# Two graph-attention layers on one core: where the fills of layer 0 end, how the first pair of heads sums its rows, and how far m^T is loaded ahead

## The chip, the cores and the metric

The kernel runs on one core of one Trainium2 chip. A core has a matrix engine (TensorE, PE in the profile, its weight loads PEld), a vector engine (VectorE, DVE), an activation engine (ScalarE, ACT), GpSimd (POOL) and a sync engine (SP) that here only issues DMAs. The engines run side by side and wait for each other on semaphores. The metric is the device time of one execution in microseconds, the median over several runs. Lower is better.

## What is computed

The input is x, eight images (B = 8) of 2048 nodes with 256 channels, and one adjacency matrix of 2048 x 2048 that all images share. Two layers follow each other, each with a residual and a layer norm. Cut to what matters:

```
def layer0(x, adj, W, a_src, a_dst, beta_tilde, W_out):     # 8 heads of width 32
    x_proj = einsum('bnd,hdf->bhnf', x, W)
    e = leaky_relu(e_src[..., :, None] + e_dst[..., None, :], 0.2)
    e = e + softplus(beta_tilde) * log(prior + 1e-6)          # prior = adj
    e = where(adj > 0, e, -max)
    h = einsum('bhij,bhjf->bhif', softmax(e), x_proj)
    return merge_heads(h) @ W_out.T

def layer1(x, adj, W1, W2, W3):
    e = leaky_relu((x @ W1) @ (x @ W2).T, 0.2)
    e = where(adj > 0, e, -1e12)
    return relu(softmax(e) @ (x @ W3))

x = layernorm(x + layer0(x, adj, ...))
x = layernorm(x + layer1(x, adj, ...))
```

All of it is computed in float32.

## The kernel before, in words

**Layer 0.** The score of a pair of nodes depends on one number of the query and one of the key, so exp(leaky_relu(...)) becomes a maximum of two products. The kernel never forms the scores. For one head and one tile of 128 keys (jt, sixteen of them) the vector engine makes a tile `s` of 128 keys x 2048 queries with one instruction: the maximum of a query row `c` and a number per key, times a tile of `m^T` (the masked adjacency factor, transposed, the same for all heads and images). That is L382. The matrix engine then multiplies `s` by the 32 columns of values of that head, which gives the numerator `val`, and by a column of key weights, which gives the row sum `den`. Both are made by `products` (L411 to L414): four matmuls side by side, each on 32 columns of the array, one for each block of 512 queries. [...] one call of `products` is eight matmul records.

The row sums can also be made on the other engines. For key tiles named in `SUMMED` (L68) there is no matmul for `den`. Instead the first of them is scaled into a tile `d` by ACT (L398), each later one is added to `d` by the vector engine (L393), and at the end of the pair one call of `products` with a tile of ones adds `d` into `den` (L405). This trades a call of `products` for a vector instruction.

The heads are taken in pairs. A unit is one key tile for one pair of heads: two `s` tiles, two calls for `val`, up to two for `den`. A pair has 16 units, an image four pairs, so 64 units. `step(count)` (L347) does `count` units. `val` and `den` have one buffer each, so the first `val` product of the next pair must wait until ACT has copied the old `val` out: eight copies (L428) and one for `den` (L430).

**Layer 1.** `Dot` works on blocks of 128 queries, sixteen for an image. A step of it transposes the weights of block it (L580, copied out by ACT, L582), makes the scores of block it+1 (L554, evicted by ACT, L556), has the vector engine apply the mask and take the maximum (L559), has ACT take the exponential (L562), and multiplies the transposed weights by `h3` into `acc` (L596). Transposes and scores share three PSUM tiles (`mm_tile`).

**How the two are put together.** The loop at the end (L684) runs layer 1 of image b-1 against layer 0 of image b. `dot.step(fill)` calls `fill(1)` after its `acc` matmuls (L597), and the fill there is a number of layer 0 units. The first pair of an image (pair 0) has its units in a fill of four (L700) and in the stretch in which the output projection of the previous image is made (L709 to L718, `output` and `turn`); that is 16 units. Two fills of two follow (L722). The remaining 44 units are spread evenly over 13 steps by the division in L725: 3, 3, 4, 3, 3, 4, 3, 4, 3, 3, 4, 3, 4. Pairs 1 and 2 therefore end inside a fill. Pair 3 ends with one.

**Loads.** The order on the matrix engine and, in this loop, on the SP queue is the order in which the program is written. The vector engine's and ACT's orders are made by the compiler's scheduler. SP issues all large loads in turn and waits at an issue until the tile's buffer is free, so what stands behind it waits too. A tile of `m^T` is 1 MB and is loaded anew for each unit (L206 to L209). Two buffers carry the tag `mt`. Two more carry the tag `d`; they hold the row-sum tiles, and in places also `m^T` tiles. `load_ahead` (L322) sets up the loads, and L386 decides after each unit whether one more is issued: two tiles ahead in general, four where a pair has no row sum chain and jt is below 12. The `s` tiles come from a ring of eight buffers, shared with the weights `p` of layer 1 and one half of the heads' output `ht`.

Of the kernel before, what the change touches and what calls it, by code (L numbers as in the profile page):

```python
# [27 lines left out]
def kernel(  # L28
# [27 lines left out]
    B, N, D = x.shape  # L56
    H, _, DH = w_proj.shape
    NT = N // P
# [5 lines left out]
    NP = H // HP  # L64
# [1 line left out]


    SUMMED = [[()] * NP, [()] + [(0, 3, 6, 8, 11, 14)] * (NP - 1)]  # L68
    SUMMED += [[(0, 4, 10, 13)] + [tuple(range(0, NT, 2))] * (NP - 1)] * (B - 2)

    const = ctx.enter_context(tc.tile_pool(name="const", bufs=1))
    dram = ctx.enter_context(tc.tile_pool(name="dram", bufs=1, space=DRAM))
# [10 lines left out]
    def ring_tile(name, shape=(P, N)):  # L83


        return wide.tile(list(shape), F32, tag="s", name=name, bufs=8)

    def wide_tile(name, tag, bufs, dtype=F32):
        return wide.tile([P, N], dtype, tag=tag, name=name, bufs=bufs)
# [113 lines left out]
        nc.sync.dma_start(mt_d[ts(jt, P), :], mt)  # L203
        return mt

    def load_mt(jt, deep):  # L206
        mt = wide_tile("mt", "d" if deep and jt % 2 else "mt", 2)
        nc.sync.dma_start(mt, mt_d[ts(jt, P), :])
        return mt  # L209

# [29 lines left out]
    class Gat:  # L240
# [81 lines left out]
        def load_ahead(self):  # L322


            self.mt_loads = (load_mt(jt, b == self.b and hp == 0)
                             for b in range(self.b, B) for hp in range(NP) for jt in range(NT))
            self.c_loads = (gats[b].query_rows(h) for b in range(self.b, B) for h in range(H))
            self.mts, self.cs_ahead = [], []
            for _ in range(HP):
                self.cs_ahead.append(next(self.c_loads))  # L330
                self.mts.append(next(self.mt_loads))
            for _ in range(2):
                self.mts.append(next(self.mt_loads))

        def follow(self, gat):
# [11 lines left out]
        def step(self, count=1):  # L347

            for _ in range(count):
                hp, jt = next(self.units)  # L350
                for work in list(self.later):
                    if next(work, self) is self:
                        self.later.remove(work)
                if hp == NP - 1 and jt == 0 and self.b + 1 < B:
                    gats[self.b + 1].load_factors()

                at = self.b * NP + hp + 1
                if at < B * NP:
                    gat = gats[at // NP]
                    if jt == 4 and gat.b > 0:  # L360
                        gat.load(at % NP)
                    elif jt == 12:
                        gat.scale(at % NP)
                if jt == 0:
                    if self.b > 0:
                        self.cs = [self.cs_ahead.pop(0) for _ in range(HP)]
                    else:
                        self.cs = [self.query_rows(hp * HP + a) for a in range(HP)]
                    self.val = pacc.tile([P, HALF], F32, tag="val", name="val")
                    self.den = pacc.tile([P, HALF], F32, tag="den", name="den")  # L370
                first = self.b == 0 and hp == 0
                if first:
                    self.more_mt(jt + 2, jt > 0)
                if self.b > 0:
                    mt = self.mts.pop(0)
                else:
                    mt = self.mts[jt] if first else load_mt(jt, True)
                s = []
                for a in range(HP):
                    h = hp * HP + a  # L380
                    sa = ring_tile("s")
                    nc.vector.scalar_tensor_tensor(sa, self.cs[a], self.re[:, 0, jt, h:h + 1], mt, ALU.max, ALU.mult)  # L382
                    s.append(sa)
                    if self.b > 0 and jt == NT - 1:
                        self.cs_ahead += [c for c in [next(self.c_loads, None)] if c]
                if self.b > 0 and len(self.mts) < (4 if not SUMMED[self.b][hp] and jt < NT - 4 else 2):  # L386
                    self.mts += [t for t in [next(self.mt_loads, None)] if t]
                v, e = self.v[hp], self.re[:, 1]
                heads = [hp * HP + a for a in range(HP)]
                chain = SUMMED[self.b][hp]  # L390
                if jt - 1 in chain[1:]:
                    for d, sa, h in zip(self.sums, self.last, heads):
                        nc.vector.scalar_tensor_tensor(d, sa, e[:, jt - 1, h:h + 1], d, ALU.mult, ALU.add)  # L393
                self.last = s
                if jt in chain[:1]:
                    self.sums = [wide_tile("d", "d", 2) for _ in heads]
                    for d, sa, h in zip(self.sums, s, heads):
                        nc.scalar.activation(d, sa, AF.Copy, scale=e[:, jt, h:h + 1])  # L398
                for a, h in enumerate(heads):
                    self.products(self.val, a, v[:, jt, ts(a, DH)], s[a], jt == 0, jt == NT - 1)  # L400
                    if jt not in chain:
                        self.products(self.den, a, e[:, jt, h:h + 1].to_broadcast([P, DH]), s[a],
                                      jt == min(set(range(NT)) - set(chain)), not chain and jt == NT - 1)
                    if chain and jt == NT - 1:
                        self.products(self.den, a, ones, self.sums[a], False, True)  # L405
                if jt == NT - 1:
                    work = self.finish(hp)
                    next(work)
                    self.later.append(work)
# [259 lines left out]
    count = (B - 1) * NT  # L669
# [14 lines left out]
    for b in range(1, B + 1):  # L684
        gat, fresh = gats[b - 1], gats[b] if b < B else None

        def layer_0(count):
            if fresh:
                fresh.step(count)

        if b > 1 and fresh:
            fresh.follow(gat)
        rows, turns = gat.output(), gat.turn()
        if dot is None:
            layer_0(4)
            next(projections)
            next(rows)
        else:

            dot.step(lambda k: layer_0((0, 4)[k]))  # L700
            if not fresh:
                for work in gat.later:
                    for _ in work:
                        pass
            next(rows)
            dot.step()
        layer_0(2)

        for g in range(NB + 2):  # L709
            if g < NB:  # L710
                next(rows)
            if g > 1:
                next(turns)
                if g == NB + 1:
                    dot = Dot(gat)
                next(turns)
            if g < NB + 1:
                layer_0(2)  # L718
        dot.scores(0)
        for _ in turns:  # L720
            pass
        dot.step(lambda k: layer_0((2, 2)[k]))  # L722
        count = NP * NT - 20
        for i in range(NT - 3):
            n = (i + 1) * count // (NT - 3) - i * count // (NT - 3)  # L725
            dot.step(lambda k: layer_0((0, n)[k]))
    dot.step()
    dot.step()
# [29 lines left out]
```

## Time and profile before

| | before |
|---|---|
| median of 3 runs | 4395.74 us (4391.2 to 4400.43) |
| the profiled execution, its own time | 4392.72 us |
| its span, first to last instruction | 4390.9 us |
| PE busy | 4163.8 us, 95% |
| DVE busy | 3697.2 us, 84% |
| ACT busy | 1714.5 us, 39% |
| DMA | 843.49 MB, mean 192 GB/s |
| mean granted TensorE clock | 0.983 |

The span has three parts. Up to about 500 us the first image goes through layer 0 alone while the projections of the other images are made. From there to about 4050 us layer 1 of one image runs against layer 0 of the next, seven times; the later rounds repeat each other every 512 us. The last 340 us are layer 1 of the last image alone, in which the vector engine is busy for a fifth of the time. A busy share is a mean over these parts. What an edit is worth is read from the part in which its instructions stand, and from the wait that ends last there. "Idle before" is time in which an engine stood still ahead of an instruction, with the instruction of the other engine that ended it.

### The profile page before, as it was taken

How to read it: one execution, taken by the hardware profiler on the slowest of the kernel's cores; microseconds unless marked ns; L12 is line 12 of the kernel's file. 1: busy time of each engine (PE TensorE's matmuls, PEld its weight loads, DVE VectorE, ACT ScalarE, POOL GpSimd, SP SyncE). 2: the span in 40 equal slices, each digit the busy share in tenths (PEclk: the TensorE clock that was granted, in tenths of full speed). 3: DMA queues.
4: the chain of work that ended last, by engine and by line, in shares of the span. 5: the costliest groups of instructions: out<-in, count | busy, mean ns of one | idle time of the engine just before them, and what ended most of it. 6: DMA issues, size and time to landing. Idle time of an engine off the chain costs nothing.

```text
span 4390.9 us, 58737 instructions
## 1 busy us (share of the span) xinstructions
PE 4163.8 (95%) x24640; PEld 2221.5 (51%) x24640; DVE 3697.2 (84%) x2468; ACT 1714.5 (39%) x3211; POOL 7.5 (0%) x14
## 2 busy tenths in 40 slices
PE   7999999999999999999999999999999999999999
PEld 4444454445545445454545445454454545455666
DVE  6878878998998989989899989989899898999222
ACT  6522243332444333343433324343333334333554
POOL 0000000000000000000000000000000000000000
PEclk9999999999999999999999999999999999999999
DMA  7988756566555555556554564555554555543211
GB/s 242 308 272 308 274 189 214 210 224 214 184 187 185 200 202 182 172 185 212 190 194 177 186 205 178 187 189 199 198 182 165 191 208 195 189 173 142 80 49 41
DMA packets 272553, 843.49 MB, mean 192 GB/s; under 512 B 33184, under 2 KB 166304, under 8 KB 198560
## 3 DMA queue, kind: packets, MB, share of 16 engines
q1 hardware_dynamic: 236448, 806.17, 52.3%
q10 hardware_dynamic: 35840, 33.57, 2.2%
q8 instruction: 193, 3.16, 0.3%
q14 instruction: 72, 0.59, 0.0%
HBM read 763.76 MB, written 75.37 MB: 191 GB/s over the span
## 4 chain that ended last, share of the span: by engine, by line
PE 62%; DVE 19%; issue 6%; ACT 6%; DMA 3%; SPq 0%; ACTq 0%; DVEq 0%
PE e L554 15%; PE acc L596 15%; PE val L414 13%; DVE s L382 11%; PE den L414 8%; DVE d L393 4%; PE pt L580 4%; ACT ht L428 3%; PE h1p L543 2%; PE y L483 2%; DMA mt<-mt_d 2%; PE proj L274 2%; DVE p L559 1%; PE h3p L522 1%; ACT d L398 1%
## 5 line engine op out<-in xcount | busy, mean ns | idle before, releaser
L382 DVE SCALAR_TENSOR_TENSOR s<-c,re,mt 128x2048 f32<-128x2048 f32 x1024 | 2360.7, 2341 | 124.6 <-DMA mt<-mt_d 52.4
L414 PE MATMUL val<-s,v 128*32 128x512 f32 x8192 | 1039.4, 609 | 122.7 <-ACT ht L428 74.1
L554 PE MATMUL e<-x1t,h 128*128 128x512 f32 x2048 | 974.1, 600 | 22.7 <-ACT pts L582 21.6
L596 PE MATMUL acc<-h,pts 128*128 128x256 f32 x4096 | 905.0, 379 | 0.0
L596 PEld LDWEIGHTS acc<-h,pts 128*128 128x128 f32 x4096 | 777.6, 190 | 156.6 <-issue 57.4
L393 DVE SCALAR_TENSOR_TENSOR d<-s,re,d 128x2048 f32<-128x2048 f32 x318 | 739.0, 2344 | 25.2 <-ACT d L398 25.2
L414 PE MATMUL den<-s,re 128*32 128x512 f32 x5216 | 684.5, 597 | 0.0
L414 PEld LDWEIGHTS val<-s,v 128*32 128x32 f32 x8192 | 243.6, 111 | 716.5 <-issue 480.4
L559 DVE CUSTOM_DVE_ANT_0 p<-p,pen 128x2048 f32<-128x2048 f32 x128 | 292.9, 2288 | 287.0 <-ACT p L556 287.0
L554 PEld LDWEIGHTS e<-x1t,h 128*128 128x128 f32 x2048 | 354.7, 192 | 287.3 <-issue 253.6
L556 ACT ACTIVATE p<-e 128x512 f32<-128x512 f32 x512 | 305.2, 596 | 432.7 <-PE e L554 424.3
L562 ACT ACTIVATE p<-p,neg 128x2048 f32<-128x2048 f32 x128 | 256.5, 2004 | 447.3 <-DVE neg L559 447.3
L580 PEld LDWEIGHTS pt<-ident,p 128*128 128x128 f32 x2048 | 249.5, 142 | 303.6 <-issue 251.8
L582 ACT COPY pts<-pt 128x512 f32<-128x512 f32 x512 | 296.4, 584 | 214.9 <-PE pt L580 201.6
L414 PEld LDWEIGHTS den<-s,re 128*32 128x32 f32 x5216 | 169.9, 111 | 393.6 <-issue 393.6
L580 PE MATMUL pt<-ident,p 128*128 128x128 f32 x2048 | 313.1, 278 | 10.4 <-ACT p L562 7.1
L230 ACT ACTIVATE f<-mv,eps_ln 128x1 f32<-128x1 f32 x128 | 37.8, 295 | 517.4 <-DVE mv L228 517.4
L428 ACT COPY ht<-val 32x512 f32<-32x512 f32 x256 | 147.8, 577 | 129.8 <-PE val L414 127.0
L601 ACT ACTIVATE z<-acc,rec 128x256 f32<-128x256 f32 x128 | 60.4, 472 | 241.0 <-PE acc L596 143.1
L274 PE MATMUL proj<-wp,xt 128*128 128x272 f32 (+1 forms) x512 | 133.7, 406 | 5.5 <-ACT both L278 2.4
L602 DVE TENSOR_TENSOR z<-z,x1r 128x256 f32<-128x256 f32 x128 | 53.9, 421 | 89.1 <-ACT z L601 89.1
L483 PE MATMUL y<-wot,ht 128*128 128x256 f32 x512 | 123.4, 396 | 1.9 <-ACT x1t L517 1.9
(88 smaller groups left out, 1980.3 us busy)
## 6 DMA issues: line engine op xcount, KB each, us to landing
mt<-mt_d SPq DMA_DIRECT2D x496, 1024.0 KB
c<-c_d SPq DMA_DIRECT2D x64, 1024.0 KB
pen<-pen_d SPq DMA_DIRECT2D x112, 512.0 KB
xg<-in_x_dram SPq DMA_DIRECT2D x60, 512.0 KB
adj_t<-in_adj_dram SPq DMA_DIRECT2D x16, 1024.0 KB
mt_d<-mt SPq DMA_DIRECT2D x16, 1024.0 KB
rb<-rec_d SPq DMA_DIRECT2D x128, 128.0 KB
x_d<-ht ACTq DMA_DIRECT2D x64, 256.0 KB
```

Of the source, the lines that this page charges most:

```text
L274: nc.tensor.matmul(t[:, 0:cols], xt[kc][:, ts(it % IG, P)], wp[:, kc, 0:cols], start=(kc == 0), stop=(kc == KC - 1))
L382: nc.vector.scalar_tensor_tensor(sa, self.cs[a], self.re[:, 0, jt, h:h + 1], mt, ALU.max, ALU.mult)
L393: nc.vector.scalar_tensor_tensor(d, sa, e[:, jt - 1, h:h + 1], d, ALU.mult, ALU.add)
L414: nc.tensor.matmul(dst[ts(q, DH), ts(a, BK)], weights, s[:, ts(q, BK)], start=start, stop=stop)
L428: nc.scalar.copy(ht[ds(lo + a * DH, DH), ts(q, BK)], self.val[ts(q, DH), ts(a, BK)])
L554: nc.tensor.matmul(t, self.h1[:, kc, ts(it % IG, P)], self.x1t[:, kc, ts(c, BK)], start=(kc == 0), stop=(kc == KC - 1))
L556: nc.scalar.activation(p[:, ts(c, BK)], t, AF.Prelu, alpha=ALPHA)
L559: nc.vector.tensor_tensor_reduce(p, p, pen, -1.0, FMAX, ALU.add, ALU.min, neg)
L562: nc.scalar.activation(p, p, AF.Exp, bias=neg, scale=-1.0, accum_out=den)
L580: nc.tensor.transpose(t[:, ts(k, P)], p[:, ts(g * IG + k, P)], ident)
L582: nc.scalar.copy(pt, t)
L596: nc.tensor.matmul(acc, pts[g][:, ts(k, P)], self.h3[:, j, :], start=(j == 0), stop=(j == NT - 1))
```

## The change

Three edits, all in the loop of rounds.

- The fills are written out as a list, 4, 4, 4, 3, 3, 3, 3, 4, 3, 3, 3, 3, 4, again 44 units in 13 steps. Now pairs 1 and 2 also end where a fill ends.
- In images 2 to 7 the first pair has no row sum chain: `SUMMED` had tiles 0, 4, 10 and 13 there. Image 1 had none in its first pair already.
- Tiles 4, 5, 8 and 9 of `m^T` of every first pair are loaded into buffers with the tag `d`, and up to four tiles are loaded ahead from jt = 2 to jt = 9. Before, this was so for image 1 alone, with every odd tile. At the start two tiles are loaded instead of four. Image 0 keeps its alternation; only the call is written otherwise.

```diff
-    SUMMED += [[(0, 4, 10, 13)] + [tuple(range(0, NT, 2))] * (NP - 1)] * (B - 2)
+    SUMMED += [[()] + [tuple(range(0, NT, 2))] * (NP - 1)] * (B - 2)
...
-    def load_mt(jt, deep):
-        mt = wide_tile("mt", "d" if deep and jt % 2 else "mt", 2)
+    def load_mt(jt, tag="mt"):
+        mt = wide_tile("mt", tag, 2)
         nc.sync.dma_start(mt, mt_d[ts(jt, P), :])
         return mt
...
-            self.mt_loads = (load_mt(jt, b == self.b and hp == 0)
+            self.mt_loads = (load_mt(jt, "d" if hp == 0 and jt in (4, 5, 8, 9) else "mt")
                              for b in range(self.b, B) for hp in range(NP) for jt in range(NT))
...
             for _ in range(HP):
                 self.cs_ahead.append(next(self.c_loads))
-                self.mts.append(next(self.mt_loads))
-            for _ in range(2):
                 self.mts.append(next(self.mt_loads))
...
-                    mt = self.mts[jt] if first else load_mt(jt, True)
+                    mt = self.mts[jt] if first else load_mt(jt, ("mt", "d")[jt % 2])
...
-                if self.b > 0 and len(self.mts) < (4 if not SUMMED[self.b][hp] and jt < NT - 4 else 2):
-                    self.mts += [t for t in [next(self.mt_loads, None)] if t]
+                if self.b > 0:
+                    ahead = 2 if hp > 0 or not 1 < jt < 10 else min(4, 11 - jt)
+                    while len(self.mts) < ahead and (mt := next(self.mt_loads, None)):
+                        self.mts.append(mt)
...
-        count = NP * NT - 20
-        for i in range(NT - 3):
-            n = (i + 1) * count // (NT - 3) - i * count // (NT - 3)
+        for n in (4, 4, 4, 3, 3, 3, 3, 4, 3, 3, 3, 3, 4):
             dot.step(lambda k: layer_0((0, n)[k]))
```

## The prediction

> **What bounds the kernel now.** I read the busy rows first (PE 95%, DVE 84%), then the chain that ended last, then the windows of one repeated round, then who waited inside it.
>
> ```profile
> PE 62%; DVE 19%; issue 6%; ACT 6%; DMA 3%; SPq 0%; ACTq 0%; DVEq 0%
> ```
>
> The chain runs mostly over PE, but a fifth of it is DVE, so the bound changes place. The rounds repeat every 512 us; one of them, from the mask (L559) of block 15 to the next block 15, in three stretches (us, then busy PE, PEld, DVE, ACT, POOL, clock, DMA share, GB/s):
>
> ```profile
> 2019.20:2140.70 121.50, 113.85 (x745) 59.26 (x747) 102.31 (x70) 39.98 (x76) 0.00 (x0) 0.99 0.63 214
> 2140.70:2254.70 114.00, 112.82 (x631) 61.15 (x624) 113.07 (x72) 40.50 (x76) 0.00 (x0) 1.00 0.50 179
> 2254.70:2531.20 276.50, 262.17 (x1512) 134.88 (x1511) 253.62 (x164) 112.15 (x197) 0.00 (x0) 0.98 0.51 184
> ```
>
> Stretch A holds most of pair 0 and the output projection: both engines have room. B1 is pair 1 up to its last units: DVE has no room (113.07 of 114) and PE hardly any. B2 is pairs 2 and 3: DVE has 23 us free, so PE and its stalls set it. PE's waits in one round (1999 to 2511):
>
> ```profile
> PE val L414 <- ACT ht L428: 10.4, 2, 7.3
> PE val L414 <- DVE s L382: 6.3, 5, 2.7
> PE e L554 <- ACT pts L582: 2.2, 1, 2.2
> PE pt L580 <- ACT p L562: 1.2, 1, 1.2
> PE den L414 <- DVE d L393: 1.2, 1, 1.2
> ```
>
> The 10.4 are the ends of pairs 1 (7.3) and 2 (3.1): the next pair's first product waits until val is copied out. The 2.2 and the 1.2 on d are the end of pair 3, which already ends a fill. The 6.3 on s all lie in A. The timeline at pair 1's end, and then at pair 3's:
>
> ```profile
> 2264.57 1.04 PE L414 MATMUL den<-d,ones 128*32 128x512 f32 x8
> ...
> 2266.15 1.99 ACT L398 ACTIVATE d<-s,re 128x2048 f32<-128x2048 f32 x1
> 2268.16 3.51 ACT L428 COPY ht<-val 32x512 f32<-32x512 f32 x6
> ...
> 2272.91 3.64 PE L414 MATMUL val<-s,v 128*32 128x512 f32 x16 [7.29 <-ACT ht L428]
> ```
> ```profile
> 2003.88 4.70 ACT L428 COPY ht<-val 32x512 f32<-32x512 f32 x8 [11.23 <-PE val L414]
> ...
> 2008.60 1.01 ACT L430 COPY dn<-den 128x1024 f32<-128x1024 f32 x1
> ...
> 2010.52 3.61 PE L554 MATMUL e<-x1t,h 128*128 128x512 f32 x4 [2.25 <-ACT pts L582]
> ```
>
> At pair 1 ACT does a 2 us scaling first and PE has nothing else. At pair 3 PE goes on to transposes and scores until its three PSUM tiles are full: the wait is shorter, not gone. Stalls cost more than their length, as the clock (the number before the last two) shows around pair 1's and pair 2's ends:
>
> ```profile
> 2260.00:2280.00 20.00, 12.71 (x86) 4.27 (x75) 14.43 (x12) 12.31 (x19) 0.00 (x0) 0.83 0.39 145
> 2400.00:2420.00 20.00, 16.89 (x93) 7.15 (x86) 17.59 (x10) 12.74 (x18) 0.00 (x0) 0.91 0.71 255
> ```
>
> A mean of 0.83 over 20 us is 6.8 us at half speed, 0.91 is 3.6; 2000 to 2020 has 0.91 as well. I charge 1.7 us of lost work for a short stall and 2 for the long one.
>
> [...] a call of products starts 0.86 us after the one before it, while its pair's eight copies take 4.7 us. [...]
>
> **The change part by part, for a round of images 2 to 7.**
>
> *Row sums of pair 0.* Removed from DVE: 3 additions x 2 heads x 2.26 us (their spacing back to back) = 13.6 us; from ACT 2 x 2.0. Added to PE: 4 tiles x 2 heads less the 2 calls with ones = 6 calls x 0.86 = 5.2 us, 31 us over six images. It all falls in A.
>
> *Stretch A.* Of the 6.3 us on s, 5.3 are two stalls, at 2059.8 and 2078.3: DVE, which has no lead, works on the projection's sums and statistics (2.5 us) between two s tiles, and twice waited 1.1 to 1.2 us for m^T. Without the additions it has 13.6 us more room, and four tiles ahead removes those m^T waits. In the built program's order DVE now makes seven s tiles beyond unit 5, behind which PE's first projection matmuls stand, before it turns to the first of those sums; before, one. So I take away 6.3 and the 1.7 of half clock after the second stall, and leave 0.3 for the unknown: 121.5 - 8.0 + 5.2 + 0.3 = 119.
>
> The deeper loads have a price on SP. Behind the pair's reciprocals SP now issues three m^T tiles before the four rb loads, where it issued one, and the third waits for the s tiles of jt = 2. The rb feed the scaling of ht (L457), behind which the output projection waits. The extra 2.1 MB take 6.8 us at the best slice's 308 GB/s; the reciprocal stands before block 15's mask now, not after it, some 4 us earlier. Net 3 us later. Against it stand 2.4 us by which ht was early (its second half scaled by 2049.3, PE's y at 2051.6), and PE's work ahead of y, 4 calls (3.4 us) longer. I take nothing, with up to 3 us.
>
> *Fills, pair 1.* After it has done its first four units, it now has three fills of four; before it was spread over one step more. B1 to its fifth mask held 43 of DVE's wide instructions, and now holds 48: five s tiles of pair 2 come forward. 114 + 5 x 2.26 = 125.3 us. PE in the same stretch: its 112.8 us of work, and pair 1's last 8 calls come forward (6.9) = 119.7, plus the wait at the pair's end. That is longer than pair 3's 2.2, since in ACT's order pts now stands behind two small layer-norm instructions that wait for DVE: 3, plus 1.7 half clock, plus 1.6 for the last d, as DVE is behind there. 126 us. Both engines say about the same; with the coupling I take 127.
>
> *Fills, pairs 2 and 3.* PE's work in B2 is 276.5 less its stalls 7.3 + 3.1 + 2.2 + 1.2 and half clocks 2 + 1.5 + 1.7 = 257.5. Less the 6.9 that went to B1: 250.6. Two aligned ends as pair 3's, each 2.2 + 1.7: 258.4. DVE there has 253.6 - 11.3 = 242 us to do, so PE still sets it. The 1.2 on d goes: in the built order the additions of tile 14 stand ahead of the s tiles of unit 15.
>
> *Sum.* 119 + 127 + 258.4 = 504.4 against 512: -7.6 a round, of which the fills give 5.1 and pair 0 gives 2.5. Six rounds: -45.6. Image 1 has no change of row sums; its fills give up to 5, but it starts with two m^T tiles instead of four, so I take 2. In all -47. Image 0 and the last image alone do not change. Against the profiled execution's own time, 4392.7: 4345.7. The median shown is 3.0 above that: **4349 us**, 1.1% faster.
>
> **Rivals.**
>
> *The wait only changes its name.* DVE binds pair 1 (113.07 of 114 speaks for it), and at the new ends PE waits for d, ACT or PSUM tiles as long as before. The fills then give nothing, pair 0 gives 2.5 x 6 = 15: 4381. Against it: B2 has room on DVE, and its ends are where most of the 10.4 lay.
>
> *The cover is complete.* Waits at all three ends fall under 1 us, and half clocks vanish: 3 x 3 = 9 us more than I take, less what DVE binds in B1, so 5 a round, 35 in all: 4314. [...] Against: the trace of pair 3's end.
>
> *Slower: rb too late.* If the three m^T tiles in front of rb delay the projection of each image by more than the 7.6 a round that is gained, the change loses. With the 2.4 us of lead that needs rb 10 us later than now; at 13 us the loss is 3 a round, 18 over six: 4413. Against: 6.8 us is the cost of the bytes, and the reciprocals come earlier.
>
> *It does not do what it says:* pair 0's additions are gone but DVE's lead was never the limit there, because val waits on the ring of s tiles; then +5.2 and no gain meets the fills' 5.1: 4395. The two named stalls speak against it.
>
> **How the numbers follow.** My case has 0.57, own range 4328 to 4370; name-changing 0.17; complete cover 0.12; slower 0.09; nothing 0.05. A difference below 0.2% (8.8 us) can't be told from none here. Faster: 0.57 + 0.12 + most of the name-changing = 0.84; same 0.07; slower 0.09. Leaving out the slower case and the outer half of the complete cover, the range is 4312 to 4386.
>
> **What will show it.** In a round of the changed kernel: val waiting on ht almost gone; e waiting on pts three times a round, 2 to 3 us each; s waits of PE in A under 1.5 us; three half-clock pieces of 3.4 us, none of 6.8; den records 64 more an image, those with ones 16 fewer; a round of 504 us. It is wrong if DVE's lag in pair 1 makes PE wait for s or d by more than 5 us, if y waits for ht in A, or if the pts waits exceed 4 us.

## The result, and the profile after

The changed kernel takes 4346.65 us, median of 4 runs (4342.52 to 4352.07), against 4393.47 for the kernel before (4 runs): a ratio of 0.9892, 95% interval 0.9873 to 0.9911. The forecast was 4349. The profiled execution took 4352.07 us with a span of 4350.3, 40.6 us less than the profiled one before.

The same three stretches of one round, cut at the same masks (L560 in the changed kernel: its lines after the diff's are higher by one, L381 is the former L382). Columns as before: length, busy PE, PEld, DVE, ACT, POOL, clock, DMA share, GB/s.

```profile
2011.20:2130.34 119.14, 115.63 (x789) 60.17 (x792) 86.23 (x64) 39.45 (x75) 0.00 (x0) 1.00 0.61 217
2130.34:2256.73 126.39, 120.84 (x688) 62.42 (x681) 124.52 (x78) 49.02 (x87) 0.00 (x0) 0.99 0.52 185
2256.73:2515.48 258.75, 254.91 (x1455) 135.31 (x1454) 245.12 (x159) 100.50 (x184) 0.00 (x0) 0.99 0.52 185
```

A is 119.1 against 121.5, B1 126.4 against 114.0 (it now holds the whole of pair 1), B2 258.8 against 276.5. Over the rounds of images 3 to 7 the sum of the three is 504.3 to 505.2 against 512. PE's waits in a round:

```profile
PE e L555 <- ACT pts L583: 7.1, 4, 3.0
PE h1p L544 <- ACT x1t L518: 1.5, 1, 1.5
PE pt L581 <- ACT p L563: 1.2, 1, 1.2
...
PE den L415 <- DVE d L394: 0.4, 1, 0.4
```

The 10.4 us of val waiting for ht and the 6.3 of val waiting for s are gone. In their place stand three waits of e for pts, one at each pair's end (3.0, 1.9 and 1.9; a fourth, elsewhere, is 0.3). This is the end of pair 1:

```profile
2242.60 2.93 ACT L429 COPY ht<-val 32x512 f32<-32x512 f32 x5
...
2245.55 1.01 ACT L431 COPY dn<-den 128x1024 f32<-128x1024 f32 x1
...
2246.46 0.30 ACT L230 ACTIVATE f<-mv,eps_ln 128x1 f32<-128x1 f32 x1
2246.66 0.19 ACT L232 ACTIVATE f<-mv 128x1 f32<-128x1 f32 x1
2246.75 0.57 ACT L583 COPY pts<-pt 128x512 f32<-128x512 f32 x1
...
2247.38 3.12 PE L555 MATMUL e<-x1t,h 128*128 128x512 f32 x4 [3.02 <-ACT pts L583]
```

PE has gone on to the transposes and the first scores and stops when its PSUM tiles are full, until ACT is through with the copies and comes to pts: 3.0 us, where the old end of pair 1 cost 7.3.

One thing went the other way. The first mask of the loop, in image 1, starts at 597.5 us instead of 590.6. PE's waits in that part (500 to 597 us):

```profile
PE val L415 <- DVE s L381: 4.7, 2, 4.4
PE y L484 <- DVE ht L458: 3.1, 1, 3.1
PE tr L517 <- DVE ht L488: 1.5, 1, 1.5
```

Before (500 to 590 us) PE had no wait of y for ht there, and less for s:

```profile
PE val L414 <- DVE s L382: 3.3, 3, 2.6
```

### The profile page after: what moved, and what is told of

Same layout as the page of the kernel before. It is cut to its first block, busy times and chain, and to the rows that moved or that the text cites. A ratio compares the mean times of both kernels' runs of the same rounds, so it can differ in the third digit from the quotient of the medians.

```text
span 4350.3 us, 59284 instructions
## 1 busy us (share of the span) xinstructions
PE 4184.8 (96%) x24928; PEld 2240.2 (51%) x24928; DVE 3617.2 (83%) x2432; ACT 1691.0 (39%) x3199; POOL 8.3 (0%) x14
## 4 chain that ended last, share of the span: by engine, by line
PE 51%; DVE 29%; issue 9%; ACT 7%; DMA 4%; SPq 0%; DVEq 0%; ACTq 0%; POOLq 0%
DVE s L381 18%; PE e L555 12%; PE acc L597 11%; PE val L415 10%; PE den L415 7%; DVE d L394 6%; PE pt L581 3%; ACT ht L429 3%; PE h3p L523 2%; DVE p L560 2%; DMA mt<-mt_d 2%; PE proj L274 2%; PE h1p L544 1%; PE y L484 1%; ACT dn L431 1%
## 5 line engine op out<-in xcount | busy, mean ns | idle before, releaser
L381 DVE SCALAR_TENSOR_TENSOR s<-c,re,mt 128x2048 f32<-128x2048 f32 x1024 | 2359.1, 2340 | 180.7 <-DMA mt<-mt_d 60.6
L555 PE MATMUL e<-x1t,h 128*128 128x512 f32 x2048 | 993.1, 610 | 57.8 <-ACT pts L583 57.4
L415 PE MATMUL val<-s,v 128*32 128x512 f32 x8192 | 1020.0, 596 | 13.7 <-DVE s L381 13.6
L415 PE MATMUL den<-s,re 128*32 128x512 f32 x5600 | 730.7, 593 | 0.0
L394 DVE SCALAR_TENSOR_TENSOR d<-s,re,d 128x2048 f32<-128x2048 f32 x282 | 653.9, 2344 | 0.0
L560 DVE CUSTOM_DVE_ANT_0 p<-p,pen 128x2048 f32<-128x2048 f32 x128 | 292.7, 2286 | 315.2 <-ACT p L557 315.2
L415 PEld LDWEIGHTS val<-s,v 128*32 128x32 f32 x8192 | 245.7, 110 | 579.4 <-issue 498.5
L415 PEld LDWEIGHTS den<-s,re 128*32 128x32 f32 x5600 | 182.3, 110 | 420.9 <-issue 420.9
L523 PE MATMUL h3p<-w3s,x1t 128*128 128x256 f32 x512 | 122.5, 383 | 9.1 <-ACT x1t L518 5.6
L544 PE MATMUL h1p<-x1t,w 128*128 128x512 f32 x256 | 119.1, 604 | 10.2 <-ACT x1t L518 10.2
## 6 DMA issues: line engine op xcount, KB each, us to landing
pen<-pen_d SPq DMA_DIRECT2D x112, 512.0 KB
xg<-in_x_dram SPq DMA_DIRECT2D x60, 512.0 KB
```

The source lines that it names most:

```text
L415: nc.tensor.matmul(dst[ts(q, DH), ts(a, BK)], weights, s[:, ts(q, BK)], start=start, stop=stop)
L555: nc.tensor.matmul(t, self.h1[:, kc, ts(it % IG, P)], self.x1t[:, kc, ts(c, BK)], start=(kc == 0), stop=(kc == KC - 1))
L560: nc.vector.tensor_tensor_reduce(p, p, pen, -1.0, FMAX, ALU.add, ALU.min, neg)
```

## The experiments

Each run is described by its edit. "B1", "B2" and "A" are measured in the profile between the starts of the masks (B1 from mask 0 to mask 5, B2 to mask 15, A to the next image's mask 0). The three columns show one round, that of the fourth image, with the A that follows its B2; most windows of A in the text are of the A ahead of it. Single rounds of one kernel differ by up to some 5 us, so "round" is the mean of four, the third to the sixth image, from mask 0 to mask 0. The last column is the ratio to the kernel before measured beside that run, with its interval.

| kernel | A | B1 | B2 | round | median us | ratio |
|---|---|---|---|---|---|---|
| before | 121.5 | 114.0 | 276.4 | 512.6 | 4393.5 | 1 |
| changed | 119.8 | 126.4 | 258.8 | 505.0 | 4346.65 | 0.9892 (0.9873 to 0.9911) |
| fills alone | 115.9 | 125.0 | 260.9 | 501.8 | 4334.35 | 0.9873 (0.9858 to 0.9887) |
| row sums alone | 122.2 | 114.4 | 277.7 | 512.7 | 4401.91 | 1.0024 (1.0013 to 1.0034) |
| row sums and loads | 118.8 | 116.5 | 276.5 | 510.3 | 4388.42 | 0.9990 (0.9982 to 0.9998) |
| fills and row sums | 118.2 | 126.4 | 257.2 | 501.7 | 4343.64 | 0.9892 (0.9876 to 0.9909) |
| changed, image 1 loaded as before | 118.7 | 126.4 | 256.4 | 503.3 | 4333.89 | 0.9870 (0.9854 to 0.9887) |
| changed, copies made twice | 120.8 | 134.3 | 260.2 | 515.3 | 4418.7 | 1.0062 (1.0042 to 1.0083) |
| changed, less chain in pair 1 | 118.3 | 128.1 | 258.6 | 505.1 | 4357.53 | 0.9921 (0.9902 to 0.9941) |
| changed, more chain in pairs 2, 3 | 119.0 | 125.0 | 261.3 | 505.3 | 4361.71 | 0.9929 (0.9910 to 0.9949) |
| changed, late chain in pair 0 | 114.0 | 126.4 | 258.2 | 498.5 | 4312.34 | 0.9816 (0.9794 to 0.9838) |
| the same, image 1 loaded as before | 113.0 | 126.4 | 259.3 | 498.5 | 4314.96 | 0.9825 (0.9809 to 0.9842) |
| the same, chain of five late tiles | 119.0 | 126.4 | 258.5 | 502.3 | 4334.57 | 0.9869 (0.9854 to 0.9884) |
| fills and late chain, loads as before | 116.3 | 126.4 | 256.7 | 499.3 | 4329.97 | 0.9870 (0.9854 to 0.9887) |

**Which part gives the gain.** First the fills by themselves, in the kernel before:

```diff
-        count = NP * NT - 20
-        for i in range(NT - 3):
-            n = (i + 1) * count // (NT - 3) - i * count // (NT - 3)
+        for n in (4, 4, 4, 3, 3, 3, 3, 4, 3, 3, 3, 3, 4):
```

> The kernel before with the new list of fills alone; row sums of pair 0 and the loads of m^T as before. Theory (the fills give the larger part, because the copies of val at the ends of pairs 1 and 2 now run beside transposes and scores): the stretch from the first mask to the fifteenth falls from 390.5 us to about 385, the stretch A stays at 121.5, so a round is 506.5 us and the whole about 4393 - 6 x 5.4 = 4360. Rival (the row sums of pair 0 give it all, the wait at the ends only changes its name): a round stays at 512, the whole at 4388 to 4393.

The fills alone give no less than the whole change: 4334.35, or 58 us (the intervals of the two ratios overlap). B1 and B2 together are 385.9, as the theory had it. But A, which should have stayed at 121.5, fell to 115.9. Its waits and its clock, from the windows and PE's waits of that run:

```profile
2012.60:2128.70 116.10, 111.98 (x745) 59.05 (x747) 99.51 (x69) 39.53 (x75) 0.00 (x0) 1.00 0.63 216
```
```profile
PE val L414 <- DVE s L382: 2.0, 3, 1.5
```

The wait for s has gone from 6.3 to 2.0 us and the half clock from A (its clock is 1.00, before 0.99), with the row sums and the loads untouched. The vector engine comes into A earlier. Pair 3 now has five steps of layer 1 beside its 16 units instead of four and two thirds, so DVE has less to do between two masks at its end. In the kernel before, the reciprocal of pair 3's row sums stands behind mask 15:

```profile
2019.20 2.29 DVE L559 CUSTOM_DVE_ANT_0 p<-p,pen 128x2048 f32<-128x2048 f32 x1 [1.57 <-ACT p L556]
...
2021.42 0.35 DVE L435 RECIPROCAL rc<-rc 128x32 f32<-128x32 f32 x1
```

With the new fills it stands in front of it:

```profile
2006.73 0.35 DVE L435 RECIPROCAL rc<-rc 128x32 f32<-128x32 f32 x1
2006.99 2.26 DVE L382 SCALAR_TENSOR_TENSOR s<-c,re,mt 128x2048 f32<-128x2048 f32 x1
2012.59 2.29 DVE L559 CUSTOM_DVE_ANT_0 p<-p,pen 128x2048 f32<-128x2048 f32 x1 [3.33 <-ACT p L556]
```

DVE is one s tile and the reciprocal further at that mask, and waits 3.3 us for it instead of 1.6. That the five steps are the reason is read off this order and was not tested by itself. There is a rival: PE's wait at pair 3's end, just ahead of A, is 5.2 us here and was 2.2 before (shown below), and DVE can use that time too. No run separates the two. Image 2 is an exception: its A is 128.4 us in this run and 119.4 before, so there the fills alone lose 9 us.

Next, the row sums by themselves, and the row sums with the loads (the changed kernel with the old division of the fills):

```diff
-    SUMMED += [[(0, 4, 10, 13)] + [tuple(range(0, NT, 2))] * (NP - 1)] * (B - 2)
+    SUMMED += [[()] + [tuple(range(0, NT, 2))] * (NP - 1)] * (B - 2)
```

> The kernel before with no row sum chain in pair 0 of images 2 to 7 alone; fills as before, m^T two tiles ahead as before. Theory: PE has 5.2 us more in stretch A, and a part of PE's waits for s stays, as m^T is late; A is 121 to 124 us, the whole 4393 to 4408, no gain. Rival (DVE was the limit in A): A falls to 119 or less, the whole to 4378 or less.

```diff
-        for n in (4, 4, 4, 3, 3, 3, 3, 4, 3, 3, 3, 3, 4):
+        count = NP * NT - 20
+        for i in range(NT - 3):
+            n = (i + 1) * count // (NT - 3) - i * count // (NT - 3)
```

> The changed kernel with the old fills: row sums and loads alone. Theory: A is as in the changed kernel, 119.8 us (-1.8 a round), the other two stretches as before (390.5), and image 1 starts 7 us later: 4393 - 11 + 7 = 4389. Rival (the deeper loads do nothing): A as in the run with the row sums alone.

Both came out as the theory said. The row sums alone are a loss of 0.24%: the wait for s falls from 6.3 to 1.1 us, but PE has its 5.2 us more and A is 122.2. With the loads A is 118.85 in each of five rounds, so with the old fills they are worth 3.4 us a round there, and the whole is level with before (-0.1%); image 1's first mask comes at 598.4.

The fourth corner is fills and row sums without the loads (both edits above in the kernel before):

> The kernel before with the new fills and no row sum chain in pair 0 of images 2 to 7, but m^T loaded as before (two tiles ahead in these images, image 1 as before). It tells what row sums and loads do once the fills are there. Theory formed after the run with the fills alone (A is bound by PE once the fills are changed, so taking the chain out costs PE's 5.2 us less the 2.0 us of waits for s that are left, and the loads then buy little): A is 119 to 121 us against 115.8 with the fills alone, the whole is 15 to 30 above that run, 4350 to 4364. Rival (the row sums still help where the fills are, and it is the deeper loads that cost): at or below the run with the fills alone, 4334.

A is 118.2, 2.3 us above the run with the fills alone; I had expected 119 to 121, and the whole to be 4350 to 4364. It was 4343.6. What I had left out is in B2: 257.2 against 260.9. Pair 3's end, with the fills alone:

```profile
1994.79 2.01 ACT L398 ACTIVATE d<-s,re 128x2048 f32<-128x2048 f32 x1 [2.28 <-DVE s L382]
1996.81 4.68 ACT L428 COPY ht<-val 32x512 f32<-32x512 f32 x8
...
2003.07 3.78 PE L554 MATMUL e<-x1t,h 128*128 128x512 f32 x4 [5.17 <-ACT pts L582]
```

and with fills and row sums:

```profile
1994.53 4.69 ACT L428 COPY ht<-val 32x512 f32<-32x512 f32 x8 [0.99 <-PE val L414]
...
2000.79 1.98 PE L554 MATMUL e<-x1t,h 128*128 128x512 f32 x4 [1.87 <-ACT pts L582]
```

With the new fills, a chain that begins with tile 0 has ACT scale that tile just where it should copy val out; PE waits 5.2 us instead of 1.9. (In the kernel before, with the same chain, ACT made the copies first and the wait was 2.2.) In the last round of the run with the fills alone, which no pair 0 follows, PE waits for pts for 3.8 us in B2 instead of 7.2. So taking the chain out gives PE 5.2 us more work in A, of which A shows 2.3, and saves 3.3 us of waiting at the end of pair 3. The round comes to 501.7 us in both runs.

The changed kernel is this run with the deeper loads, and its round is 505.0. PE's waits are the same in both (3.8 us in B2, 3.5 in A). What differs is the clock: 1.00 in B2 here, 0.99 in the changed kernel, whose B2 has two pieces of 3.4 us at half clock in each of these rounds (from 2377.79 and from 2507.50 us in this one):

```profile
2254.58:2511.73 257.15, 253.33 (x1464) 135.26 (x1463) 244.91 (x158) 100.04 (x184) 0.00 (x0) 1.00 0.53 187
```

So the 3.2 us a round are not work or waits that the loads add; the last section comes back to them.

**The start of image 1.** The changed kernel, with image 1's loads put back:

```diff
-            self.mt_loads = (load_mt(jt, "d" if hp == 0 and jt in (4, 5, 8, 9) else "mt")
+            self.mt_loads = (load_mt(jt, "d" if hp == 0 and (jt % 2 if b == self.b else jt in (4, 5, 8, 9)) else "mt")
...
+            for _ in range(2):
+                self.mts.append(next(self.mt_loads))
...
-                if self.b > 0:
+                if self.b == 1:
+                    if len(self.mts) < (4 if hp == 0 and jt < NT - 4 else 2):
+                        self.mts += [t for t in [next(self.mt_loads, None)] if t]
+                elif self.b > 0:
```

> The changed kernel with the m^T loads of image 1 as before (four tiles at the start, every odd one in a d buffer, one load a unit), images 2 to 7 as changed. Theory (image 1 pays 7 us because it starts with two tiles and its rb loads stand behind three m^T loads): the first mask is back at 590.6 us from 597.6, and the whole is 7 us below the changed kernel, 4340. Rival (the 7 us come from the fills or are the order of other work): no difference, 4347.

The first mask is back at 589.1 us. The 7 us are image 1's loads. On SP, the first rb loads of image 0 are issued at 497.2 in the changed kernel, behind three m^T tiles, and at 489.0 before, behind one:

```profile
486.93 1.74 SPq L208 DMA_DIRECT2D mt<-mt_d  x3
497.19 1.73 SPq L452 DMA_DIRECT2D rb<-rec_d  x4
```
```profile
488.35 0.57 SPq L208 DMA_DIRECT2D mt<-mt_d  x1
489.02 2.03 SPq L451 DMA_DIRECT2D rb<-rec_d  x4
```

Between 478 and 557 us DVE waits for m^T five times, 6.9 us in all, and before not once; PE's output projection waits 3.1 us for ht. The second is the mechanism of my slower rival, in the one image where nothing covers it. The run put all loads of image 1 back at once, so it does not tell how much of the 7 us is rb and how much the two m^T tiles fewer at the start. The rest of the gain (the median is 12.8 us below the changed kernel's) is in rounds whose instructions are the same in both kernels (503.3 us on the mean against 505.0); see the last section. The intervals of the two ratios overlap.

**Which engine sets B1 and B2.** I had said DVE for B1 and PE for B2. Two runs move work between them in one stretch each:

```diff
-    SUMMED += [[()] + [tuple(range(0, NT, 2))] * (NP - 1)] * (B - 2)
+    SUMMED += [[()] + [tuple(range(0, NT - 2, 2))] + [tuple(range(0, NT, 2))] * (NP - 2)] * (B - 2)
```

> The changed kernel with tile 14 taken out of the row sum chain of pair 1 in images 2 to 7: DVE 4.5 us less and PE 1.7 us more in B1. Theory (DVE binds B1, busy 124.5 of 126.4 us): B1 falls by 1 to 2.5 us, the whole by 6 to 15: 4332 to 4341. Rival (PE binds B1): B1 grows by 1.7, the whole by 10: 4357.

```diff
-    SUMMED += [[()] + [tuple(range(0, NT, 2))] * (NP - 1)] * (B - 2)
+    SUMMED += [[()] + [tuple(range(0, NT, 2))] + [tuple(range(0, NT, 2)) + (13,)] * (NP - 2)] * (B - 2)
```

> The changed kernel with tile 13 added to the row sum chains of pairs 2 and 3 in images 2 to 7: PE 3.4 us less and DVE 9 us more in B2, where DVE has 13.6 us free. Theory (PE binds B2): B2 falls from 258.6 to about 255.5, the whole by 18 to 4329. Rival (DVE is bound there too, its free time lies where it can't be used): no change or slower, 4347 to 4365.

Both went the rival's way. With 4.5 us less on DVE, B1 grew by 2.1 us on the mean of five rounds (1.3 to 2.8); the calls added to PE are 1.7 of it. With 3.4 us less on PE, B2 grew by 2.5. The windows of the two stretches, B1 of the first run and B2 of the second:

```profile
2129.92:2258.04 128.12, 121.65 (x700) 62.42 (x693) 122.85 (x77) 49.80 (x87) 0.00 (x0) 0.99 0.52 185
```
```profile
2261.01:2522.26 261.25, 252.47 (x1422) 134.42 (x1421) 251.45 (x161) 100.18 (x184) 0.00 (x0) 0.98 0.52 184
```

DVE was busy for 98.5% of B1 in the changed kernel and still did not set it. A reason can be read from the trace: it comes to B1 with two units of s tiles done, after standing still for 18.5 us ahead of mask 0. In B2 of the second run PE's waits are

```profile
PE e L555 <- ACT pts L583: 6.4, 2, 4.6
PE den L415 <- DVE d L394: 2.3, 1, 2.3
```

against 3.8 and none in the changed kernel. Both lie at the ends of the pairs: at pair 3's the addition of tile 13 makes the last d late, and at pair 2's the wait for pts rises from 1.9 to 4.6. With 1.7 us more of half clock (reckoned from B2's clock, 0.98 against 0.99 in the changed kernel) these outweigh the 3.4 us of calls saved. So the run speaks against my reading that DVE has room for more additions there, for a tile this late in the pair. That DVE sets B2 as a whole is not shown, and an earlier tile was not tried.

The other test of the ends doubles the copies:

```diff
                     nc.scalar.copy(ht[ds(lo + a * DH, DH), ts(q, BK)], self.val[ts(q, DH), ts(a, BK)])
+                    if b > 0:
+                        nc.scalar.copy(ht[ds(lo + a * DH, DH), ts(q, BK)], self.val[ts(q, DH), ts(a, BK)])
```

> The changed kernel, where in images 1 to 7 each of the eight copies of val at the end of a pair is made twice: 4.7 us more on ACT at each end, the same output. Theory (at an aligned end PE runs on until its three PSUM tiles are full and then waits for ACT, so there is no cover left): each of the three ends costs PE the full 4.7 us and somewhat more half clock; pair 0's end 3 to 4; a round is longer by 15 to 20 us, the whole by 100 to 130: about 4460. Rival (transposes and scores cover the copies, the waits seen are something else): below 30 us more.

It fell between the two: 72 us more, 10.3 a round. The edit is not clean: each second copy came after its first, and at pair 1 the scheduler put a 2.0 us scaling and layer norm work between them, so 16 copies of 0.57 us took 14 us. There PE's wait grew from 3.0 to 11.3 us and B1 by 7.9. In B2, at the ends of pairs 2 and 3, PE's waits for pts grew from 3.8 to 7.5 us, but B2 only by 1.5. There the waits came in six pieces of at most 1.5 us, and B2 had no half clock (its clock is 1.00; the changed kernel's, with two pieces of 3.4 us, is 0.99).

**A better place for the chain.** DVE stands still in the second half of A, where the d buffers are no longer needed for m^T:

```diff
-    SUMMED += [[()] + [tuple(range(0, NT, 2))] * (NP - 1)] * (B - 2)
+    SUMMED += [[(10, 12, 14)] + [tuple(range(0, NT, 2))] * (NP - 1)] * (B - 2)
```

> The changed kernel with a row sum chain of tiles 10, 12 and 14 in pair 0 of images 2 to 7, that is after the d buffers are free of m^T: 4 calls of products (3.4 us) fewer on PE, 4 additions (9 us) more on DVE, in a stretch in which DVE stands still for 18.5 us ahead of the mask. Theory (A is bound by PE in the changed kernel): A falls from 119.8 to about 116.5, the whole by 20 to 4327. Rival (DVE or ACT set A, so that the chain was taken out for good reason): no change or slower, 4347 to 4360.

A falls from 119.8 to 114.0 (113.0 to 115.3 over five rounds), and the whole to 4312.34, 1.8% below the kernel before. PE's waits for s and d are absent from A, and taking calls from PE shortened it, so PE sets A in the changed kernel:

```profile
2003.40:2116.40 113.00, 110.76 (x751) 57.91 (x753) 94.81 (x67) 43.42 (x77) 0.00 (x0) 1.00 0.65 229
```

On the mean of five rounds A falls by 5.3 us: 3.4 are the calls, and PE's other waits in A fall from 3.5 to 2.2. Together with image 1's old loads:

> The changed kernel with the row sum chain of tiles 10, 12 and 14 in pair 0 and with image 1's loads of m^T as before: the two runs that each gained, together. If they add up: the first mask at 589 to 591 us instead of 601, A about 114, the whole 4312 - 10 = 4302. If they share one gain: 4312 or above.

The first mask is at 590.4 instead of 601.1, but the median is 4314.96: the two do not add up beyond what the runs can tell. Then five late tiles instead of three:

> As the run before this one, with a chain of the five tiles 10 to 14: PE 4 calls (3.4 us) less, DVE 4 additions (9 us) more, within the 18.5 us in which it stood still ahead of the mask in the changed kernel. Theory (PE binds A until DVE's free time is used up): A falls by 2 to 3.4 us more, the whole to about 4287. Rival (the lead of DVE at the start of pair 1 is what carries B1, and the chain eats it): A or B1 grows, 4302 or above.

The rival was right: A is 119.0 (117.3 to 119.0 over five rounds, a mean of 118.1 against 114.2). PE waits for DVE again, in the stretch from 2510.4 to 2629.4:

```profile
PE val L420 <- DVE s L383: 2.7, 1, 2.7
PE den L420 <- DVE d L399: 2.6, 1, 2.6
```

DVE still stands still for 10.5 us ahead of the next mask: its time was not used up, the additions came where PE needed s and d.

Last, the late chain with the fills but with m^T loaded as before:

> The kernel before with the new fills and, in pair 0 of images 2 to 7, a row sum chain of tiles 10, 12 and 14 instead of 0, 4, 10 and 13; loads of m^T as before. Theory (with the fills in place the early chain costs at pair 3's end, where ACT's scaling of tile 0 stands ahead of the copies and PE waits 5.2 us instead of 1.9, and the deeper loads buy nothing): B2 about 258 us as in the run without a chain, A about 115, a round about 498.5, the whole 4343.6 - 20 = 4323 or less; if the deeper loads cost the 1 to 2 us a round that they cost beside no chain, 4305 to 4312. Rival (the late chain needs m^T four tiles ahead): A 118 or more, the whole 4335 or above.

4329.97: neither. B2 is 256.7 as expected, A 116.3 (114.1 to 116.3), and image 2's first A is 124.6 against 116.9 with the deeper loads. The loads of images 2 to 7 are worth some 15 us beside the late chain (4329.97 against 4314.96, the intervals of the ratios apart). In the profiles most of it lies in image 2; the later rounds are 499.3 and 498.5 us. Beside no chain it is 10 us (fills and row sums, 4343.64, against the changed kernel with image 1 loaded as before, 4333.89), which the intervals don't tell from none; but there too image 2's A falls, from 128.1 to 120.3. So what the loads buy beside the new fills is to take back what the fills lose in image 2.

## Why the prediction was right, and where its working was not

**The sum held.** 4349 was forecast, 4346.65 measured; -47 us against the profiled execution, -40.6 in the profile after. By stretch, forecast and measured: A 119 and 119.8, B1 127 and 126.4, B2 258.4 and 258.8. Six rounds: -45.6 forecast, -47.3 in the profile (from the second image's first mask to the end). Image 1: -2 forecast, +6.7 in the profile. (45.6 and 2 make 47.6; the -47 of the forecast was rounded down.)

**The ends of the pairs: right.** The wait of pair 1's end was worked out as 3 and is 3.02, those of pairs 2 and 3 as 2.2 and are 1.9. The 7.3 and 3.1 are gone. The 1.2 on d at pair 3's end is gone as forecast, and at pair 1's end, where 1.6 was allowed for the last d, it is 0.4. The half clock came out as charged, three pieces of 3.4 us a round, but that is in part luck: with fills and row sums the three waits are the same, and the clock in the round of the fourth image is 1.00 in A, 0.99 in B1 and 1.00 in B2, which is one piece. The charge of 1.7 us for each short stall was one outcome of several.

**Stretch A: the term that failed.** The step "I take away 6.3 and the 1.7 of half clock" is right as an effect and was put down to the wrong edit. The fills alone take most of it away. The row sums then add to PE in A what they save at pair 3's end, and the loads then buy nothing in these rounds. So the fills give 10.2 us a round (512 to 501.7) and not 5.1, and the other two edits together cost 3.2 a round on top of the fills in the changed kernel's profile, instead of giving 2.5. (Where image 1 alone is loaded otherwise the same two cost 1.5, and the mean clock is 0.990 against the changed kernel's 0.988, so part of this is the clock.) The forecast of the whole came out because the two errors, 5.1 and 5.7 us a round, almost cancel: that is luck. What I had missed is that the list of fills also changes how far DVE is ahead when it enters A, be it by the steps that stand beside pair 3 or by PE's longer wait at its end. I had looked at the fills' list for pairs 1 to 3 alone.

**What binds B1 and B2: wrong in name for B1, open for B2, right in length.** I leaned on DVE for B1 (113.07 of 114 busy) and took PE for B2. For B1 the run that shifts work says PE. Both engines' sums lay within 2 us of the stretch's length there, so either gave the number. For B2, taking calls from PE brought nothing, because the additions in their place made PE wait at the ends of the pairs. I had counted DVE's instructions (242, and 245 measured) and not when in a pair they come due.

**SP's queue: the size was right for the rounds and not for image 1.** In the rounds the rb loads cost nothing, as I took: y does not wait for ht there. In image 1, for which I allowed 3 us against 5 of gain, they and the two missing m^T tiles cost 7.

**The rivals.** "The wait only changes its name" fell: val's 10.4 us are gone, and the waits for pts at the two new ends are 4.9. "The cover is complete" fell with the three waits that are left. The slower rival was there in image 1 alone. That the row sums bring nothing in A came closest to the truth of the parts: the row sums alone do lose. Its reason did not hold, since the wait for s does fall with them, from 6.3 to 1.1.

## What to carry to other kernels

When two loops are interleaved, the place where one of them changes its accumulator is the place to put the other's work, and the gain is the wait that was, less the wait at the next shared resource (here 10.4 us a round for val at the ends of pairs 1 and 2, less 4.9 for PSUM tiles behind ACT's copies; B1 and B2 together fell by 5.4). Moving that place also moves how much work each engine has around it, so look for the effect in the neighbouring stretches too. An engine that is 98% busy in a stretch may still not set it, if it enters with a lead (DVE in B1: 124.5 of 126.4 us, two units ahead); shift a known amount of work off it, and see whether the stretch follows. And a sum that comes out does not show that its terms are right: here the run with the fills alone undid two of them.

## What the runs showed of the hardware

A round made of the same instructions does not always take the same time, and the granted TensorE clock goes with the difference. In the profiles of the kernel before and of the changed kernel it is either 1.00 or 0.50 at any time. In the changed kernel, for one, it is 1.00 from 2240.00 to 2248.08 us, 0.50 from there to 2251.49, and 1.00 again up to 2377.79, where the next piece at half clock begins. From 100 us on, 24 of the pieces in the changed kernel are 3.41 us long and one is 6.83; in the kernel before 24 are 3.41, seven are 6.83 and one is 10.24. (The last piece of each trace, close to its end, is left out: 5.03 and 3.13.) In each of the two profiles it is a whole number of steps of 3.413 us from the start of one to the start of any other: the starts at 2248.08, 2377.79 and 2507.50 in the changed kernel, for one, are twice 129.71 us apart, or 38 steps.

B1, with the same instructions and the same waits, takes 124.99, 126.41 or 127.67 us. Its clock is 1.00, 0.99 or 0.97 in them; reckoned from that, they hold none, one and two pieces of 3.41 us (the late chain, fills and row sums, and the changed kernel with image 1 loaded as before):

```profile
1621.01:1746.00 124.99, 119.44 (x688) 61.54 (x681) 124.58 (x78) 48.88 (x87) 0.00 (x0) 1.00 0.51 186
2128.17:2254.58 126.41, 120.87 (x688) 62.16 (x681) 124.53 (x79) 49.07 (x87) 0.00 (x0) 0.99 0.53 185
3128.73:3256.40 127.67, 122.14 (x688) 62.89 (x681) 124.53 (x78) 49.18 (x87) 0.00 (x0) 0.97 0.52 187
```

The stall in them is the same, 3.0 us at pair 1's end. Why it goes with none, one or two pieces was not shown. So whether such a stall costs only itself, or 1.3 to 1.4 us more for each piece, is not settled by its length.

Where a round repeats well it lies near a whole number of these steps of 3.413 us: before, 511.9 (150 steps are 512.0); fills alone and fills with row sums, 501.7 (147 are 501.8); the changed kernel, 505.0, and more chain in pairs 2 and 3, 505.2 (148 are 505.2); copies made twice, 515.3 (151 are 515.4). The late-chain kernels' rounds wander between 495 and 502 us. My estimate from these lengths is that rounds can settle on whole steps. Then a saving of 1 or 2 us a round would show as nothing or as 3.4, and two kernels that differ in image 1 alone could differ in later rounds, as two did here (503.3 and 505.0). No run was made to test this settling; the agreement of the lengths is all that stands for it.
